# A graph-attention and expert-layer kernel: the fourth block loaded among the first, chains of blocks 3 and 4 begun at turns 8 and 12, padding and biases written ahead of the first slots

## The chip, the core and the metric

The kernel runs on one core of a Trainium2 chip (trn2). The metric is the device time of one execution in microseconds. The profile's engines are PE (TensorE matmuls), PEld (TensorE weight loads), DVE (VectorE), ACT (ScalarE), POOL (GpSimd) and SP (SyncE, which issues most DMAs).

## The reference

Two layers over x of shape (128, 64, 256), 128 graphs of 64 nodes, with an adjacency per graph. Each layer is an attention over the nodes of a graph and then a layer of 8 experts of which each token takes two. Cut to what matters:

```python
# layer l; ln is a layer norm without weights
xn = ln(x); Wh = xn @ W
e  = (Wh @ a1)[:, :, None] + (Wh @ a2)[:, None, :]     # layer 1: leaky relu on e
att = softmax(where(adj > 0, e, -9e15))
x  = x + elu(att @ Wh)
t  = ln(x)
logits = t @ router                                     # layer 1: + bg + bias
w, idx = top2(logits), softmax over the two
# layer 0: x = x + (t + sum over the two experts of w * (gelu(t @ w1 + b1) @ w2 + b2))
# layer 1: x = x + sum over the two experts of w * (relu(t @ w1 + b1) @ w2 + b2)
```

The hidden width of an expert is 256 in layer 0 and 512 in layer 1. All data is fp32.

## The kernel before

The 8192 tokens are cut into 16 blocks of 512 tokens (TT = 4 tiles of 128 rows, 8 graphs) for each layer, so `blks` has 32 entries. A block passes through two Python generators that issue instructions up to each `yield`.

`attend` (blocks `a`): statistics of the layer norm on DVE (L225 to L228), the power `rs` on POOL (L230), the mask `cap` from the adjacency on POOL (L277), the normalised `xn` on ACT (L238), its transposes `pt` on PE (L249) and their copies `xt` (L253 on DVE, L255 on ACT), `pw` and its copy `wh` (L288, L295), `sm` (L299), the scores `pe` and `ee` (L307 to L323), the exponentials (L326), their division, the transposes `pp` and copies `pT` (L339, L340), the product `po` and its exponential `ex` (L346, L354), and `xb` (L360, L363).

`route` (blocks `r`): statistics again, `tn` (L238), its transposes, the router's product `pl` (L417), the copy `lg` (L426), the two largest, the residual scaled in place (L433) and written to `mid` by a DMA that POOL issues (L437), the position `ix` of each token in the list of its two experts (L477 to L492), eight scatters of rows to `lists` in HBM, issued by POOL (L497), and the `plan` of the next slots (L537 to L594).

A slot is 256 rows of one expert's list. `fetch` loads it (`xg`, L609), `weights` loads the expert's weights and biases (`wc`, L651, L655, L659, the last from `bcat`), and the slot's `x` (transposes L680, copy L684), `h` (L749, L757) and `y` (L777, L785, a scatter to `res` at L791) do the expert's work. `rest_of_lists` writes padding rows at the end of the lists (eight DMAs a layer, L850). `gather_biases` loads a layer's biases to `tb` (L206, L212) and `put_biases` writes them to `bcat` (L218).

The order is written out by hand. PE, DVE, ACT and SP run their instructions in the order in which the program issues them (`manual_schedule` over `ORDERED`); POOL's order is chosen by the framework, and each engine runs its own queue in order. The start loads blocks 0 to 2, then runs a loop of turns: in each turn, each chain whose turn has come issues its next stage. A chain of a block has 11 entries of attention (12 stages) and then the stages of the route:

```python
chains = [
    (0, att(0)[3:] + [(r, 0)] * 10),
    (1, att(1)[2:] + [(r, 1)] * 10),
    (2, att(2) + [(r, 2)] * 10),
    (11, att(FIRST) + [(r, FIRST)] * 2),
    (20, [(a, FIRST + 1)] * 3),
]
```

With FIRST = 3, block 0's `ix` is issued at turn 15 and its scatters at turn 16; those of blocks 1 and 2 follow at turns 17/18 and 20/21. Behind the turns `slots.fetch()` loads the first four slots, and the main loop over blocks begins, in which the stages of three blocks and the slots are interleaved. Tiles come from pools with a number of buffers for each tag; a tile of a tag waits until the buffer that it takes has been read for the last time. The tag `xs` has 3 buffers, `yb` (which `tb` uses too) has 2, `cap`, `ee` and `adj` have 3.

Of the kernel before, what the change touches and what calls it, by code (L numbers as in the profile page):

```python
# [8 lines left out]
F32 = mybir.dt.float32  # L9
I32 = mybir.dt.int32  # L10
# [6 lines left out]
P = 128  # L17
NG = 64
D = 256
KD = D // P  # L20
E = 8
TT = 4
# [13 lines left out]
def adj_ffn_kernel(  # L36
# [40 lines left out]
    FIRST = 3  # L77
# [11 lines left out]
    work = ctx.enter_context(tc.tile_pool(name="work", bufs=3))  # L89
# [21 lines left out]
    def part(b):  # L111

        return int(b >= CUT)
# [10 lines left out]
    for g in range(2):  # L124
        r = slice(g * NG, (g + 1) * NG)
# [30 lines left out]
    def load_gw(l):  # L156
        gw.append(const.tile([P, KD, D + 2], F32, name=f"gw{l}"))
        av.append(const.tile([P, KD, 2], F32, name=f"av{l}"))
        nc.sync.dma_start(
            out=gw[l][:, :, 0:D], in_=gnn_w[l].rearrange("(k p) f -> p k f", p=P)  # L160
        )
        nc.sync.dma_start(out=av[l], in_=gnn_a[l])

    def make_gw(l):
        wt = work.tile([P, KD, D], F32, tag="xt", name=f"wt{l}", bufs=2)
        for o in range(KD):
            pt = ps_c.tile([P, D], F32, tag="a", name=f"pwt{l}_{o}")
            for k in range(KD):
                nc.tensor.transpose(
                    pt[:, k * P : (k + 1) * P], gw[l][:, k, o * P : (o + 1) * P], ident  # L170
                )
            nc.scalar.copy(wt[:, o, :], pt)
        for k in range(KD):
            pa = ps_c.tile([P, 2], F32, tag="a", name=f"pa{l}_{k}")
            for o in range(KD):
                nc.tensor.matmul(
                    pa,
                    lhsT=wt[:, o, k * P : (k + 1) * P],
                    rhs=av[l][:, o, :],
                    start=(o == 0),  # L180
                    stop=(o == KD - 1),
                )
            nc.scalar.copy(gw[l][:, k, D : D + 2], pa)
# [4 lines left out]
    def load_router():  # L188
        for l in range(2):
            nc.sync.dma_start(out=rw[l], in_=router[l].rearrange("(k p) e -> p k e", p=P))  # L190
        nc.sync.dma_start(out=gb2[:, 0, :], in_=bg.partition_broadcast(P))
        nc.sync.dma_start(out=gb2[:, 1, :], in_=gbias.partition_broadcast(P))

    def counted(name, shape, pattern, base, mult):
        ti = work.tile(shape, I32, tag="cap", name=f"{name}_i")
        nc.gpsimd.iota(ti, pattern=pattern, base=base, channel_multiplier=mult)
        t = const.tile(shape, F32, name=name)
        nc.vector.tensor_copy(t, ti)
        return t

    def gather_biases(l):

        tb = work.tile([P, E, D + HC[l]], F32, tag="yb", name=f"tb{l}", bufs=2)
        nc.sync.dma_start(  # L206
            out=tb[:, :, 0:D],
            in_=b2[l].rearrange("e d -> (e d)").partition_broadcast(P).rearrange(
                "p (e d) -> p e d", e=E
            ),  # L210
        )
        nc.sync.dma_start(out=tb[:, :, D : D + HC[l]], in_=b1[l])  # L212
        if l == 0:
            nc.vector.tensor_scalar(tb[:, :, 0:D], tb[:, :, 0:D], -2.0, None, ALU.add)
        return tb

    def put_biases(l, tb):
        nc.sync.dma_start(out=bcat[l].rearrange("e p d -> p e d"), in_=tb)  # L218
# [611 lines left out]

    def load_block(l, b, first=None):

        xs = work.tile([P, TT, D], F32, tag="xs", name=f"xs{l}_{b}")
        yb = None
        nc.sync.dma_start(out=xs, in_=(mid_t if l else x_t)[b])
        if first:
            first()
        if l:
            yb = work.tile([P, TT, 2 * D], F32, tag="yb", name=f"yb{l}_{b}", bufs=2)
            nc.sync.dma_start(out=yb, in_=res_t[part(b)][b])  # L840
        ai = work.tile([P, TT, NG], I32, tag="adj", name=f"adj{l}_{b}")
        nc.sync.dma_start(out=ai, in_=adj_t[b])
        return xs, yb, ai


    def rest_of_lists(l):

        for e in range(E):
            r = E * CAP + e * SL
            nc.sync.dma_start(  # L850
                out=lists[l][r : r + SL, :].rearrange("(t p) d -> p t d", p=P),
                in_=pad[:, :, 0 : ROW[l]],
            )

    slots = Slots()
    blks = [{"l": l, "b": b} for l in range(2) for b in range(NB)]

    def there(i):
        return 0 <= i < len(blks) and blks[i]

    def load(i, first=None):
        if there(i):
            k = blks[i]
            if k["l"]:
                assert all(s["l"] or s["part"] != part(k["b"]) for s in slots.all[slots.ny :])
            k["in"] = load_block(k["l"], k["b"], first)
            k["a"] = attend(k["l"], k["b"], k)

    def a(i, n=1):
        if there(i):  # L870
            for _ in range(n):
                next(blks[i]["a"], None)

    def r(i, n=1):
        if there(i):
            k = blks[i]
            if "r" not in k:
                k["r"] = route(k["l"], k["b"], k)
            for _ in range(n):
                next(k["r"], None)  # L880
# [5 lines left out]
    load(1)  # L886
    load(2)
    load_router()
    a(0, 2)
    make_gw(0)  # L890
    a(0)
    a(1, 2)
    token2 = counted("token2", [P, NT], [[2 * P, NT]], 0, 2)
    token = counted("token", [P, NT], [[P, NT]], 0, 1)
    place = counted("place", [P, ST], [[P, ST]], 0, 1)
    att = lambda b: [(a, b)] * 9 + [(a, b, 2), (a, b)]
    chains = [
        (0, att(0)[3:] + [(r, 0)] * 10),
        (1, att(1)[2:] + [(r, 1)] * 10),
        (2, att(2) + [(r, 2)] * 10),  # L900
        (11, att(FIRST) + [(r, FIRST)] * 2),
        (20, [(a, FIRST + 1)] * 3),
    ]
    turn = 0
    while any(c for _, c in chains):
        for first, chain in chains:
            if turn >= first and chain:
                stage, *what = chain.pop(0)
                stage(*what)
        if turn == 2:  # L910
            places = counted("places", [P, SL], [[1, SL]], 0, 0)
            steps = counted("steps", [P, KS], [[SL, KS]], 0, 0)
            snum = counted("snum", [P, SF], [[1, SF]], 0, 0)
            tb0 = gather_biases(0)
        if turn == 5:
            put_biases(0, tb0)
            load_gw(1)
        if turn in (6, 8, 11):
            load(FIRST + (turn - 6) // 2)
        if turn == 11:  # L920
            make_gw(1)
        turn += 1
    slots.fetch()
    for t in range(FIRST, len(blks)):
        n = t + 1
        more = slots.nf - slots.ny > SB or len(slots.all) - slots.ny > SB
        if t + 3 != NB:
            load(t + 3)
        if t == FIRST:
            put_biases(1, gather_biases(1))  # L930
            rest_of_lists(0)
        if t == FIRST + 1:
            rest_of_lists(1)
        a(n)
        h()
        x()
        a(n)
        r(t - 1)
        a(n)
        h()  # L940
        r(t)
        slots.fetch()
        if more:
            x()
        a(n)
        r(t)
        if t + 2 != NB:
            a(t + 2)
        y()
        a(n)  # L950
        (h if more else x)()
        r(t)
        a(n)
        y()
        a(t + 2, 1 + (t + 2 == NB))
        if more:
            x()
        a(n)
        r(t)
        h()  # L960
        a(n)
        if more:
            y()
        x()
        a(n)
        h()
        r(n)
        y()
        a(t + 2)
        r(t)  # L970
        r(t)
        y()
        slots.fetch()
        x()
        r(n)
        r(t)
        if t + 3 == NB:
            load(t + 3)
# [57 lines left out]
```

## Time and profile before

| what | value |
|---|---|
| time, median of 3 runs | 1467.6 us (1464.61 to 1468.28) |
| the profiled execution's own time | 1464.47 us |
| its span | 1462.6 us |
| mean granted TensorE clock | 0.956 |
| DMA | 315.42 MB, mean 216 GB/s |
| scatters to `lists` (L497) | 256, mean 975 ns |
| first and last scatter of blocks 0 to 2 | 77.72 and 108.36 us |
| first fetch of slots (L609) | 110.99 us |
| first expert matmul (L749) | 138.66 us |

The profile is of one execution; its times are microseconds from the start of the span. A matmul's line has its output tile, its inputs, and its shape; the text in brackets at the end of a line of the timeline is how long the engine had been idle and what it waited for. PE is busy for 86% of the span; in the first 111 us it is busy for 66.86 us.

### The profile page before, as it was taken

How to read it: one execution, taken by the hardware profiler on the slowest of the kernel's cores; microseconds unless marked ns; L12 is line 12 of the kernel's file. 1: busy time of each engine (PE TensorE's matmuls, PEld its weight loads, DVE VectorE, ACT ScalarE, POOL GpSimd, SP SyncE). 2: the span in 40 equal slices, each digit the busy share in tenths (PEclk: the TensorE clock that was granted, in tenths of full speed). 3: DMA queues.
4: the chain of work that ended last, by engine and by line, in shares of the span. 5: the costliest groups of instructions: out<-in, count | busy, mean ns of one | idle time of the engine just before them, and what ended most of it. 6: DMA issues, size and time to landing. Idle time of an engine off the chain costs nothing. (4 is left out here: it accounts for less than half of the span.)

```text
span 1462.6 us, 22822 instructions
## 1 busy us (share of the span) xinstructions
PE 1264.9 (86%) x6436; PEld 1082.9 (74%) x6436; DVE 885.6 (61%) x3404; ACT 670.3 (46%) x1567; POOL 767.8 (52%) x742
## 2 busy tenths in 40 slices
PE   6646789889989888888889999899988998899996
PEld 4534677777777777777778887777877787688885
DVE  3663777776677678677766655666566655423332
ACT  5523556546655554545444444344444443233232
POOL 3261566656565555555563654555645465544333
PEclk9766999989999999999999999999999999999999
DMA  4228766697666779777786987898877778987773
GB/s 128 83 98 266 240 209 219 210 279 233 214 216 210 268 253 271 260 240 235 240 254 183 265 238 205 220 263 223 228 195 215 209 193 212 241 248 215 214 178 57
DMA packets 267199, 315.42 MB, mean 216 GB/s; under 512 B 41400, under 2 KB 224319, under 8 KB 267073
## 3 DMA queue, kind: packets, MB, share of 16 engines
q1 hardware_dynamic: 222240, 227.80, 51.3%
q0 software_dynamic: 44832, 86.17, 22.0%
q8 instruction: 51, 0.84, 0.2%
q14 instruction: 76, 0.61, 0.1%
HBM read 215.03 MB, written 102.51 MB: 217 GB/s over the span
## 5 line engine op out<-in xcount | busy, mean ns | idle before, releaser
L749 PE MATMUL ph_s<-xT_s,wc_s 128*128 128x256 f32 x1760 | 418.9, 388 | 71.1 <-DVE xT_s L684 49.3
L749 PEld LDWEIGHTS ph_s<-xT_s,wc_s 128*128 128x128 f32 x1760 | 333.4, 193 | 135.1 <-DVE xT_s L684 66.6
L777 PE MATMUL py_s<-wc_s,hT_s 128*128 128x256 f32 x1760 | 417.1, 387 | 14.9 <-issue 14.6
L777 PEld LDWEIGHTS py_s<-wc_s,hT_s 128*128 128x128 f32 x1760 | 331.4, 193 | 59.9 <-issue 17.2
L820 POOL DMA_INDIRECT out_dram<-ys_s,to_s x142 | 223.1, 1571 | 273.2 <-ACT ys_s L817 170.3
L497 POOL DMA_INDIRECT lists<-tn_r,ix_r x256 | 249.5, 975 | 110.9 <-issue 66.1
L757 ACT ACTIVATE hT_s<-ph_s,wc_s 128x256 f32<-128x256 f32 x440 | 182.3, 469 | 176.8 <-PE ph_s L749 88.1
L785 DVE TENSOR_TENSOR ys_s<-py_s,wc_s 128x512 f32<-128x512 f32 x149 | 102.9, 691 | 196.1 <-PE py_s L777 184.5
L791 POOL DMA_INDIRECT res<-ys_s,to_s x156 | 159.0, 1019 | 117.4 <-DVE ys_s L785 51.6
L684 DVE COPY xT_s<-px_s 128x512 f32<-128x512 f32 x149 | 102.3, 686 | 118.1 <-PE px_s L680 118.1
L817 ACT ACTIVATE ys_s<-ys_s,cf_s 128x256 f32<-128x256 f32 x142 | 64.1, 499 | 141.1 <-DVE ys_s L785 134.8
L288 PE MATMUL pw_g<-gw,xt_g 128*128 128x258 f32 x512 | 125.5, 395 | 1.7 <-ACT wh_g L295 1.3
L288 PEld LDWEIGHTS pw_g<-gw,xt_g 128*128 128x128 f32 x512 | 95.8, 196 | 22.8 <-ACT xt_g L255 6.3
L238 ACT ACTIVATE xn_g<-xs,nb_g,rs_g 128x256 f32<-128x256 f32 x128 | 66.4, 589 | 82.0 <-DVE nb_g L236 82.0
L238 ACT ACTIVATE tn_r<-xb_g,nb_r,rs_r 128x256 f32<-128x256 f32 x128 | 66.4, 589 | 66.8 <-DVE nb_r L236 66.8
L680 PE MATMUL px_s<-ident,xg_s 128*128 128x128 f32 x596 | 90.9, 276 | 0.5 <-DMA xg_s<-lists 0.5
L680 PEld LDWEIGHTS px_s<-ident,xg_s 128*128 128x128 f32 x596 | 74.9, 145 | 13.0 <-DMA xg_s<-lists 0.6
L277 POOL TENSOR_SCALAR cap_g<-adj 128x256 f32<-128x256 int32 x32 | 35.7, 1117 | 91.6 <-DMA adj<-in_adj_dram 90.2
L346 PE MATMUL po_g<-wh_g,pT_bd 128*128 128x256 f32 x256 | 69.0, 417 | 7.4 <-ACT pT_bd L340 5.8
L295 ACT COPY wh_g<-pw_g 128x258 f32<-128x258 f32 x128 | 47.7, 374 | 54.2 <-PE pw_g L288 53.2
L417 PEld LDWEIGHTS pl_r<-rw,xt_r 128*128 128x128 f32 x512 | 68.1, 207 | 2.9 <-DVE xt_r L253 0.6
L230 POOL TENSOR_TENSOR rs_r<-ve_r,nhalf 128x4 f32<-128x4 f32 x32 | 38.3, 1198 | 57.1 <-DVE ve_r L228 50.4
(474 smaller groups left out, 1597.8 us busy)
## 6 DMA issues: line engine op xcount, KB each, us to landing
wc_s<-in_w_dram SPq DMA_DIRECT2D x142, 512.0 KB, 4.3
wc_s<-in_w_dram SPq DMA_DIRECT2D x156, 256.0 KB, 3.9
xg_s<-lists SPq DMA_DIRECT2D x78, 258.0 KB, 4.3
xg_s<-lists SPq DMA_DIRECT2D x71, 260.0 KB, 4.4
yb<-res SPq DMA_DIRECT2D x16, 1024.0 KB, 10.5
wc_s<-bcat SPq DMA_DIRECT2D x78, 129.0 KB, 3.8
wc_s<-bcat SPq DMA_DIRECT2D x71, 130.0 KB, 5.3
xs<-in_x_dram SPq DMA_DIRECT2D x16, 512.0 KB, 6.1
```

Source lines behind the costliest of these rows:

```text
L238: nc.scalar.activation(outs(t), xb[:, t, :], AF.Identity, bias=nb[:, t : t + 1], scale=rs[:, t : t + 1])
L288: nc.tensor.matmul(pw, lhsT=xt[:, k, t * P : (t + 1) * P], rhs=gw[l][:, k, :], start=(k == 0), stop=(k == KD - 1),)
L346: nc.tensor.matmul(po[h][:, j, :], lhsT=pT[:, 2 * h + j, :], rhs=wh[:, 2 * h + j, 0:D], start=True, stop=True,)
L497: ins = nc.gpsimd.indirect_dma_start(out=lists[l], out_offset=bass.IndirectOffsetOnAxis(ap=ix[:, k, t : t + 1], axis=0), in_=tn[:, t, 0 : ...
L680: nc.tensor.transpose(px[:, c, t * P : (t + 1) * P], xg[:, t, c * P : (c + 1) * P], ident)
L684: nc.vector.tensor_copy(xT, px)
L749: nc.tensor.matmul(ph[:, j, :], lhsT=wc[:, o : o + P], rhs=xT[:, c, :], start=(c == 0), stop=(c == KD - 1),)
L757: nc.scalar.activation(hT[:, f + j, :], ph[:, j, :], AF.Gelu if l == 0 else AF.Relu, bias=wc[:, OB1[l] + f + j : OB1[l] + f + j + 1],)
L777: nc.tensor.matmul(py[:, t, :], lhsT=hT[:, f, t * P : (t + 1) * P], rhs=wc[:, O2[l] + f * D : O2[l] + (f + 1) * D], start=(f == 0), stop=( ...
L785: nc.vector.tensor_tensor(ys, py, wc[:, OB2[l] : OB1[l]].unsqueeze(1).to_broadcast([P, ST, D]), ALU.add)
L791: ins = nc.gpsimd.indirect_dma_start(out=res[sl["part"]], out_offset=self.row(sl, t), in_=ys[:, t, :], in_offset=None, bounds_check=2 * N - 1,
L820: ins = nc.gpsimd.indirect_dma_start(out=out, out_offset=self.row(sl, t), in_=ys[:, t, :], in_offset=None, compute_op=ALU.add,)
```

## The change

Block 3's input and adjacency are loaded behind the first three blocks' instead of at turn 6; its `xs` takes a buffer of the tag `yb`. Blocks 4 and 5 are loaded at turns 6 and 8 (before: 8 and 11). The chain of block 3 begins at turn 8 instead of 11, that of block 4 at turn 12 instead of 20. The last stage of block 2's route (its plan) is issued behind the turns. The biases of layer 1 are loaded and written at turn 5, and the padding of both layers at turn 11; before, both stood in the first two rounds of the main loop. The weights of the first four slots are issued straight behind the first fetch (`slots.ahead()`). The small integer tiles of `counted` take buffers of `ee` instead of `cap`.

```diff
     def counted(name, shape, pattern, base, mult):
-        ti = work.tile(shape, I32, tag="cap", name=f"{name}_i")
+        ti = work.tile(shape, I32, tag="ee", name=f"{name}_i")
...
     def load_block(l, b, first=None):
-        xs = work.tile([P, TT, D], F32, tag="xs", name=f"xs{l}_{b}")
+        tag, bufs = ("yb", 2) if l == 0 and b == FIRST else ("xs", 3)
+        xs = work.tile([P, TT, D], F32, tag=tag, name=f"xs{l}_{b}", bufs=bufs)
...
     load(2)
     load_router()
+    load(FIRST)
...
-        (2, att(2) + [(r, 2)] * 10),
-        (11, att(FIRST) + [(r, FIRST)] * 2),
-        (20, [(a, FIRST + 1)] * 3),
+        (2, att(2) + [(r, 2)] * 9),
+        (8, att(3) + [(r, 3)] * 2),
+        (12, [(a, 4)] * 3),
...
-            tb0 = gather_biases(0)
+            tb = gather_biases(0)
         if turn == 5:
-            put_biases(0, tb0)
+            put_biases(0, tb)
             load_gw(1)
-        if turn in (6, 8, 11):
-            load(FIRST + (turn - 6) // 2)
+            tb = gather_biases(1)
+            put_biases(1, tb)
+        if turn in (6, 8):
+            load(4 + (turn - 6) // 2)
         if turn == 11:
             make_gw(1)
+            for l in range(2):
+                rest_of_lists(l)
         turn += 1
+    r(2)
     slots.fetch()
+    slots.ahead()
...
-        if t == FIRST:
-            put_biases(1, gather_biases(1))
-            rest_of_lists(0)
-        if t == FIRST + 1:
-            rest_of_lists(1)
```

## The prediction

> **What bounds the kernel now.** I read the page first, then a table by stage, the list of waits, and the timeline of the start.
>
> ```profile
> span 1462.6 us, 22822 instructions
> PE 1264.9 (86%) x6436; PEld 1082.9 (74%) x6436; DVE 885.6 (61%) x3404; ACT 670.3 (46%) x1567; POOL 767.8 (52%) x742
> ```
>
> TensorE carries the kernel. By stage (columns: stretch, length, busy time of PE, PEld, DVE, ACT, POOL, granted clock, DMA share, GB/s):
>
> ```profile
> 0.00:111.00 111.00, 66.86 (x268) 50.99 (x268) 59.47 (x251) 49.00 (x126) 48.82 (x102) 0.77 0.34 103
> 111.00:150.00 39.00, 27.44 (x112) 20.83 (x113) 17.34 (x67) 16.30 (x39) 5.90 (x7) 0.70 0.93 278
> 200.00:400.00 200.00, 177.90 (x934) 151.30 (x933) 145.46 (x562) 113.40 (x251) 124.90 (x126) 0.97 0.77 239
> ```
>
> From 200 us on PE is busy 89% of the time; the first 150 us leave it idle for 56 us. Only this start is changed; behind it the order on every engine is the same in both kernels, and nothing is tied to absolute time. So the change is worth the shift of one fixed point: the first expert matmul, ph of slot 0, at 138.66. The waits in 95 to 140 us (engine, line, waited for: us, times, longest):
>
> ```profile
> PE pt_g L249 <- ACT xn_g L238: 13.6, 1, 13.6
> PE ph_s L749 <- DMA wc_s<-in_w_dram: 6.4, 1, 6.4
> POOL mid L437 <- ACT xb_g L433: 5.4, 1, 5.4
> ```
>
> The timeline (start, duration, what) shows how these arise:
>
> ```profile
> 67.66 0.19 DVE L426 COPY lg_r<-pl_r 128x32 f32<-128x32 f32 x1 [1.86 <-PE pl_r L417]
> ...
> 77.72 1.11 POOL L497 DMA_INDIRECT lists<-tn_r,ix_r  x1 [5.26 <-DVE cs L466]
> ...
> 108.36 0.96 POOL L497 DMA_INDIRECT lists<-tn_r,ix_r  x1 [0.30 <-issue]
> ...
> 109.34 1.05 POOL L230 TENSOR_TENSOR rs_g<-ve_g,nhalf 128x4 f32<-128x4 f32 x1
> ...
> 110.99 3.07 SPq L609 DMA_DIRECT2D xg_s<-lists  x4
> ...
> 114.01 5.67 PE L288 MATMUL pw_g<-gw,xt_g 128*128 128x258 f32 x16
> ...
> 123.65 9.29 SPq L850 DMA_DIRECT2D lists<-pad  x8
> ...
> 128.47 3.78 PE L346 MATMUL po_g<-wh_g,pT_bd 128*128 128x256 f32 x8 [1.84 <-ACT pT_bd L340]
> ...
> 138.66 3.38 PE L749 MATMUL ph_s<-xT_s,wc_s 128*128 128x256 f32 x8 [6.40 <-DMA wc_s<-in_w_dram]
> ```
>
> GpSimd issues 24 scatters of blocks 0 to 2, one each 1.27 us, from 77.72 to 109.3 (24 x 1.27 = 30.5, and one write of mid). Block 4's rs (L230) stands behind them, so xn and PE wait: the 13.6 us. Then SP has block 6's loads, tb1, bcat1 and eight pads ahead of the first weights, which leave at 134.15: the 6.4 us.
>
> **The change, part by part.** *Early load of block 3.* xs3 and adj3 go out at about 9.6 and 10 us instead of 37.36; they delay tb0 by 0.66 MB, about 3 us at 222 GB/s. tb0 was down by 15 and its L214 ran at 19.36: 0. The load was not late before either (its first reader ran at 63.4). What it buys is that the xs buffers freed at 37.3 and 45.1 now go to blocks 4 and 5.
>
> *tb1 and bcat1 early.* tb1 takes tb0's buffer, so SP stands until bcat0 has landed (issued 20.60; the DMA rate falls after 25), then about 6 us as tb0 took: bcat1 leaves at 32 to 33. Behind it on SP is xs4, which waits for its buffer until 37.3 anyway: 0; each us past 37.3 would hold adj4 and with it cap4 and rs of block 0 on POOL.
>
> *Sixteen pads at 46 us,* behind adj5. They hold SP until some 62 us and the DMA for 4.1 MB / 0.3 MB per us = 14 us; nothing else there is urgent but adj5, which cap5 needs and behind which rs of blocks 3 and 1 stand on POOL. adj loads land in 3.9 us; 6.1 are free before DVE would wait. [...] the pads' own landings under saturation were 5.9 and 7.6 in the median, 8.0 at most, which would cost 1.9. I take 0, bounds 0 and 1.9. On GpSimd the iotas in other buffers let cap2 move ahead of rs of block 1: about 1 us late, with 4 us of room before its xn at 17.84: 0.
>
> *Chains 3 and 4 at turns 8 and 12.* This is the cost. The first scatter needs ix of block 0 (turn 15). Ahead of it now stand block 3's stages to exp (before: to its transposes) and block 4's statistics and xn. Walking the queues from 48.6, where the two orders part:
> - DVE: block 3's statistics first (2.4), so pT of block 2 is at 53.4 instead of 52.24. ACT: then xn of block 3 (2.07) ahead of tn of block 1 and ex of block 2: ex at 60.4 instead of 58.85, the first L360 done at 61.7.
> - PE from 61.75: block 3's transposes 2.1, make_gw 2.4 (as at 60.20), pt_r 1.4, pw of block 3 4.9 (as at 77.48), pl of block 1 1.85 (with gaps): ends at 74.4 instead of 67.63.
> - DVE waits for that pl, then works without a pause: lg group 1.3, statistics of blocks 2 and 4 at 2.42 each, sm 0.45, c group 0.58, second choice 1.59, nb 0.3, ee and emx 0.9, at to ix 2.1: 12.1. ix at 86.5, first scatter at **86.6: 8.9 late**.
>
> *What this buys.* rs of block 4 is ahead of all scatters and rs of block 3 behind 16 of them: 86.6 + 20.4 + one write of mid 1.1 = 108.1. DVE stands there at nb of block 3 (109.3), then does the plan (3.7): xt of block 4 at 113.2, pw at 113.95, as before (114.01). So the 13.6 us wait only moves. Scatters end at 86.6 + 32.7 = 119.3, the fetch leaves at 121.0, slot 0 lands 4.1 later: px at 125.1 instead of 123.4. But DVE reached xT only at 125.37 before; now 125.75, so po ends at 132.7. Weights leave from 124.4 and land by 129.6. ph starts at **132.7**: 6.0 earlier. All is the removed weight wait.
>
> *The clock.* In windows of ten us the clock was
>
> ```profile
> 50.00:60.00 10.00, 9.01 (x34) 7.61 (x33) 3.15 (x15) 6.64 (x13) 2.75 (x3) 0.52 0.15 52
> 130.00:140.00 10.00, 3.60 (x9) 2.43 (x8) 1.71 (x4) 1.41 (x4) 1.03 (x1) 0.50 1.01 292
> ```
>
> [...] By it the dense stretch from 61.75 runs at full rate (pw 3.83, pl 1.85, pt 1.04): pl ends at 72.3, first scatter 84.4, and ph of slot 0, behind po without a gap, takes 1.99 instead of 3.38: 8.2 + 1.4 = 9.6 gained. The row at 50 to 60 speaks against it: 9.0 us busy, clock 0.52. Were all of it so (pt 2.31, pw 5.67, pl 3.42), pl ends at 78.0, first scatter 90.2, gain 2.4. I take the middle walk and half of the 1.4: **6.7 us gained**.
>
> The tail of r(2) behind the loop is the same instructions; the fetch needs the scatters, 6 us after the plan: 0. The second eight pads leave the stretch from 143, where PE was 0.9 busy: 0.
>
> The sum is against the profiled execution: 1464.5 (span 1462.6 and 1.9 around it) to 1457.8. That is one of the fast ones; the median of the three is 1467.6, so I forecast 1467.6 - 6.7 = **1460.9**. A difference of 0.3% (4.4 us) is about what a measurement of this kernel can tell from no change.
>
> **Rivals.** *B, the early stages are hidden.* From 40 to 77 us (the windows of ten us added up) PE was idle for about 11 us, ACT for 16 and DVE for 14. If they fit into that, the first scatter stays near 77.7 and ph comes at 77.7 + 46.1 = 123.8: 14.9 + 1.4 = 16.3 gained, 1451.3. Against it: the queues are in order, and pw stands in front of pl.
>
> *C, the gain is given back.* The half clock of the row at 50 to 60, or a late ix of block 1 (slack 1.2 us to its scatters): 0 to 4.4 gained, about 1465.
>
> *D, slower: none of it is hidden.* The added stages ahead of ix of block 0 at full latency: statistics and rs 3.4, xn and transposes 2.9, xt 0.7, pw 5.3, sm 0.45, pe 1.2, ee and emx 0.9, exp 2.1, block 4's statistics, rs and xn 5.5: 22.4. First scatter at 100, ph at 146: 7.5 lost, 1475. It decides from a first scatter at 97.0. For it: POOL, DVE and ACT hand each stage on, so latencies count. Against it: much of block 4's part is not read in that stretch.
>
> *E, the change does not do what it says.* Chains 3 and 4 do start earlier on all queues, but the load is no cure: the transfer of block 3 was hidden already. That is inside A and C.
>
> **How the numbers follow.** A (4.4 to 10 gained) 0.50; B and between (over 10) 0.17; C 0.20; D 0.13. Faster 0.67, same 0.20, slower 0.13. A's own range is 1457 to 1463. The range for 8 in 10 takes in B's end and C: 1451 to 1467; outside are D and a little beyond B.
>
> **What would show it.** First L497 at 84 to 90 instead of 77.72; last one at 117 to 123; PE idle before pt or pw of block 4 still above 10 us; no wait of ph on wc; ph of slot 0 at 130 to 134; pads at 46 to 62. I am wrong if the first scatter stays below 82 or passes 92, if POOL waits for adj5 beyond 51.7, or if ph shifts by 6 us and the span does not.

## The result and the profile after

| | before | after |
|---|---|---|
| time, median | 1468.09 us (5 runs, 1464.61 to 1471.29) | 1455.54 us (5 runs, 1452.59 to 1456.64) |
| the profiled execution's own time | 1464.47 us | 1454.15 us |
| its span | 1462.6 us | 1452.2 us |
| mean granted TensorE clock | 0.956 | 0.960 |

The ratio is 0.9918, with a 95% interval of 0.9903 to 0.9934: about 12 us faster, 10 to 14 by the interval. A second comparison of the changed kernel, run with the last experiments, gave 1454.64 us (5 runs, 1453.25 to 1457.95) against 1467.24, ratio 0.9920 (0.9906 to 0.9935). The forecast was 1460.9 us, in a range of 1451 to 1467.

The head of the page of the changed kernel, and PE's longest wait in its first 140 us (engine, line, waited for: us in total, times, longest):

```profile
span 1452.2 us, 22826 instructions
PE 1264.1 (87%) x6436; PEld 1083.9 (75%) x6436; DVE 884.4 (61%) x3404; ACT 670.1 (46%) x1567; POOL 767.2 (53%) x742
```

```profile
PE pw_g L288 <- DVE xt_g L253: 13.0, 1, 13.0
```

No engine does less work; PE's busy time differs by 0.8 us in 1264. The 13 us wait of PE for block 4 is still there and only has another name: pw waits for xt on DVE, where pt waited for xn. The 6.4 us wait of ph for the weights is gone from the list. The timeline of the changed kernel shows both:

```profile
46.62 13.31 SPq L852 DMA_DIRECT2D lists<-pad  x16
...
74.28 0.19 DVE L426 COPY lg_r<-pl_r 128x32 f32<-128x32 f32 x1 [8.59 <-PE pl_r L417]
...
85.91 1.10 POOL L497 DMA_INDIRECT lists<-tn_r,ix_r  x1 [4.17 <-DVE ix_r L492]
...
107.03 1.05 POOL L230 TENSOR_TENSOR rs_r<-ve_r,nhalf 128x4 f32<-128x4 f32 x1
...
108.12 0.16 DVE L236 SCALAR_TENSOR_TENSOR nb_r<-mv_r,rs_r 128x4 f32<-128x4 f32 x1 [2.40 <-POOL rs_r L230]
...
112.98 6.16 PE L288 MATMUL pw_g<-gw,xt_g 128*128 128x258 f32 x16 [13.02 <-DVE xt_g L253]
...
117.19 0.96 POOL L497 DMA_INDIRECT lists<-tn_r,ix_r  x1 [0.30 <-issue]
...
119.98 3.09 SPq L609 DMA_DIRECT2D xg_s<-lists  x4
...
123.62 0.38 SPq L651 DMA_DIRECT2D wc_s<-in_w_dram  x1
...
127.80 3.78 PE L346 MATMUL po_g<-wh_g,pT_bd 128*128 128x256 f32 x8 [1.85 <-ACT pT_bd L340]
...
131.37 1.99 PE L749 MATMUL ph_s<-xT_s,wc_s 128*128 128x256 f32 x8
```

Before, SP issued the biases (from 115.17) and eight pads between the fetch and the weights:

```profile
115.17 0.50 SPq L206 DMA_DIRECT2D tb<-in_b_dram  x1
...
134.15 0.40 SPq L651 DMA_DIRECT2D wc_s<-in_w_dram  x1
```

Everything up to the fetch is later than before: the first scatter by 8.2 us (77.72 to 85.91), the fetch by 9.0 (110.99 to 119.98). Yet the weights leave 10.5 us earlier (134.15 to 123.62), since neither biases nor padding lie between the fetch and them, and ph of slot 0 starts at 131.37 instead of 138.66, straight behind po and with no wait of its own. That is 7.3 us. It also took 1.99 us instead of 3.38, at a mean granted clock of 0.95 instead of 0.58 over its run. At slot 1 the changed kernel is 8.7 us ahead, at the last slot 10.3, which is the difference of the two spans (10.4).

### The profile page after: what moved, and what is told of

Read it like the earlier page. It is cut to its first block, busy times and chain, and to the rows that moved or that the text cites. A ratio compares the mean times of both kernels' runs of the same rounds, so it can differ in the third digit from the quotient of the medians.

```text
span 1452.2 us, 22826 instructions
## 1 busy us (share of the span) xinstructions
PE 1264.1 (87%) x6436; PEld 1083.9 (75%) x6436; DVE 884.4 (61%) x3404; ACT 670.1 (46%) x1567; POOL 767.2 (53%) x742
## 5 line engine op out<-in xcount | busy, mean ns | idle before, releaser
L288 PEld LDWEIGHTS pw_g<-gw,xt_g 128*128 128x128 f32 x512 | 96.7, 197 | 35.1 <-issue 13.2
L417 PE MATMUL pl_r<-rw,xt_r 128*128 128x8 f32 x512 | 63.5, 259 | 2.9 <-ACT xt_r L255 2.5
## 6 DMA issues: line engine op xcount, KB each, us to landing
yb<-res SPq DMA_DIRECT2D x16, 1024.0 KB, 10.2
```

The costliest lines, as they stand in the source:

```text
L288: nc.tensor.matmul(pw, lhsT=xt[:, k, t * P : (t + 1) * P], rhs=gw[l][:, k, :], start=(k == 0), stop=(k == KD - 1),)
L417: nc.tensor.matmul(pl[:, t, :], lhsT=tT[:, k, t * P : (t + 1) * P], rhs=rw[l][:, k, :], start=(k == 0), stop=(k == KD - 1),)
```

## Experiments

All were timed in five rounds beside runs of the kernel before on the same chip. The table gives the end points; "shift" is how far ahead of the profile of before the copy xT of a slot stands (slot 1, and the last; slots are counted from 0). Each profile is of one execution, so a shift need not match its ratio: the profile of the writes only took 1461.37 us, where the median is 1456.54.

| kernel | ratio (95% interval) | first scatter | weights leave | ph of slot 0 | shift, us |
|---|---|---|---|---|---|
| before | 1 | 77.72 | 134.15 | 138.66 | 0, 0 |
| changed | 0.9918 (0.9903 to 0.9934) | 85.91 | 123.62 | 131.37 | 8.7, 10.3 |
| changed, again | 0.9920 (0.9906 to 0.9935) | 86.71 | 124.26 | 132.10 | 8.0, 9.8 |
| writes only | 0.9915 (0.9893 to 0.9938) | 79.41 | 116.25 | 132.99 | 6.0, 3.2 |
| chains only | 1.0045 (1.0028 to 1.0062) | 86.19 | 143.03 | 150.25 | -12.4, -10.4 |
| biases only | 0.9921 (0.9898 to 0.9943) | 77.86 | 124.44 | 132.55 | 7.5, 8.9 |
| padding only | 0.9920 (0.9900 to 0.9941) | 77.89 | 114.50 | 131.08 | 8.1, 8.6 |
| weights first | 0.9933 (0.9912 to 0.9954) | 84.80 | 111.37 | 132.92 | 6.8, 11.1 |
| block 4 ahead | 0.9975 (0.9962 to 0.9988) | 85.45 | 109.68 | 132.94 | 5.1, 0.6 |
| block 3 at turn 9 | 0.9890 (0.9870 to 0.9911) | 82.13 | 121.14 | 128.07 | 10.9, 11.4 |
| block 3 at turn 10 | 0.9903 (0.9878 to 0.9927) | 84.70 | 122.78 | 129.50 | 10.6, 12.2 |
| block 4 early | 0.9896 (0.9881 to 0.9911) | 81.12 | 120.73 | 124.70 | 13.2, 11.8 |
| block 4 early, weights first | 0.9920 (0.9907 to 0.9934) | 80.98 | 108.60 | 125.06 | 11.2, 11.8 |

### The two halves of the change apart

Writes only: the kernel before, with the biases, the padding and the first weights where the changed kernel has them (the padding at turn 8, not 11), and its own loads and chains.

```diff
         if turn == 5:
             put_biases(0, tb0)
             load_gw(1)
+            put_biases(1, gather_biases(1))
+        if turn == 8:
+            for l in range(2):
+                rest_of_lists(l)
...
     slots.fetch()
+    slots.ahead()
...
-        if t == FIRST:
-            put_biases(1, gather_biases(1))
-            rest_of_lists(0)
-        if t == FIRST + 1:
-            rest_of_lists(1)
```

> Before, with only the writes moved: biases of layer 1 at turn 5, padding of both layers at turn 8, first weights straight behind the first fetch; load and chains of blocks 3 and 4 as before. Theory W (the moved writes carry the gain, the early chains none of it): first list scatter at 77 to 79 us, the wait of PE for block 4's xn of some 13 us stays, no wait of ph on wc, ph of slot 0 at 131 to 133 us, time 8 to 11 us below before (ratio 0.9925 to 0.9945). Rival C (the early chains carry it): ph of slot 0 above 135 us and at most 3 us gained.

Chains only: the changed kernel with exactly these writes put back into the main loop, and no `slots.ahead()` behind the fetch.

> After, with the writes put back where before has them (biases of layer 1 and padding in the first rounds of the main loop, weights behind them); block 3 loaded early and chains 3 and 4 at turns 8 and 12. Theory W: first list scatter at 86 us, fetch at 120, then block 6's loads, biases, eight pads on SP, so that the first weights leave at about 143 and ph of slot 0 comes at 147 to 149: 8 to 10 us slower than before (ratio about 1.006). Rival C: ph of slot 0 below 133, 5 us or more gained.

Measured: 1456.54 us for the writes, 1474.78 for the chains, against 1467.66. The timeline of the kernel with the writes only, from PE's wait for block 4 to ph:

```profile
112.85 2.80 PE L249 MATMUL pt_g<-ident,xn_g 128*128 128x128 f32 x8 [13.60 <-ACT xn_g L238]
...
132.99 3.00 PE L749 MATMUL ph_s<-xT_s,wc_s 128*128 128x256 f32 x8
```

The same 13.6 us wait as before, and ph has none. The waits and the timeline of the kernel with the chains only:

```profile
PE ph_s L749 <- DMA wc_s<-in_w_dram: 18.4, 1, 18.4
```

```profile
134.01 7.97 SPq L852 DMA_DIRECT2D lists<-pad  x8
...
143.03 0.40 SPq L651 DMA_DIRECT2D wc_s<-in_w_dram  x1
...
150.25 3.78 PE L749 MATMUL ph_s<-xT_s,wc_s 128*128 128x256 f32 x8 [18.44 <-DMA wc_s<-in_w_dram]
```

So all of the gain is the writes', and the early chains alone lose 6.6 us (0.0045 of 1467.7). The two runs also show why the loss does not show in the whole change. Where the queue behind the fetch sets ph, the chains' delay of the fetch (9.6 here, 120.60 against 110.99) reaches ph: it came 11.6 later, since the weights left 8.9 later and took 2.7 longer from there to ph. With the writes away, ph is set by PE's own chain, pw of block 4 to po, and the place of pw hardly moves with the chains (its rs stood behind 24 scatters, and now nb of block 3 stands behind 16 later ones): pw starts at 114.01, 112.98, 113.74 and 113.60 in before, changed, changed again and chains only. A delay of the fetch is then covered.

### Which of the writes

Biases only moves the line `put_biases(1, gather_biases(1))` of the kernel before to turn 5 and nothing else. Padding only moves both layers' padding to turn 8, and the first weights behind the fetch:

```diff
+        if turn == 8:
+            for l in range(2):
+                rest_of_lists(l)
...
     slots.fetch()
+    slots.ahead()
...
         if t == FIRST:
             put_biases(1, gather_biases(1))
-            rest_of_lists(0)
-        if t == FIRST + 1:
-            rest_of_lists(1)
```

> The kernel before with only the biases of layer 1 (gather and put) at turn 5; padding, weights, loads and chains as before. Theory W (the weights were 6.4 us late behind 18.9 us of bias and padding issues, so taking away either part of 8.5 us or more ends the wait): weights leave at about 125.7 (134.15 before), the first ph at 132 to 133 with no wait or one under 1 us, time 5 to 7 us below before, as with both parts moved but for the second layer's padding. Rival (the two parts each carry their share of the gain): ph at 135 to 136, time about 3 us below before.

> The kernel before with only the padding of both layers at turn 8, and the weights issued ahead of the main loop, behind the first fetch; biases of layer 1, loads and chains as before. bcat of layer 1 then stands behind the weights of the first slots for the layer 0, and only its own wait is left for what follows. Theory W: weights leave at about 116, the first ph at 132 to 133 with no wait, time 5 to 8 us below before, within 3 us of the kernel that moves both. Rival (the biases' wait of 5.2 us ahead of bcat then stops the queue in front of the next weights or the next fetch): ph of slot 0 without a wait but that of a later slot with one, and less than half of the gain left by slot 8.

Measured: 1456.52 and 1456.98 us against 1468.31. Moving the biases alone gives the whole gain. The second run gives it too, but it does not take the padding alone out of the way: `slots.ahead()` puts the first weights in front of the biases as well. It shows that the biases cost nothing once they stand behind these weights; what moving the padding alone would bring was not run. SP's queue with the biases moved, and then ph:

```profile
118.19 5.04 SPq L850 DMA_DIRECT2D lists<-pad  x8
...
124.44 0.39 SPq L651 DMA_DIRECT2D wc_s<-in_w_dram  x1
...
132.55 1.97 PE L749 MATMUL ph_s<-xT_s,wc_s 128*128 128x256 f32 x8
```

The wait to be removed was 6.4 us, and each half holds more: from the first bias DMA to the first pad SP spent 8.5 us (115.17 to 123.65), and from the first pad to the weights 10.5 (123.65 to 134.15). Once ph stands behind po, taking more out of SP's queue buys nothing: weights at 114.50 or at 124.44 give ph at 131.08 and 132.55. In the kernel with the padding moved, the biases' stop of 6 us (bcat1 leaves at 133.19, the loads before it were issued by 127.16) stands behind the weights and holds up block 7's load and nothing that is waited for: the shift is 8.1 us at slot 1 and 8.2 at slot 20. The rival, that it comes back in a later slot, is refuted.

### What is last in the changed kernel

Weights first: the changed kernel with `slots.ahead()` in front of `slots.fetch()`.

> After, with the first four slots' weights issued ahead of the first fetch. Theory W and Q: the weights are already down when ph of slot 0 becomes ready behind po of block 4, so ph stays at 131 and the time within 1.5 us of after. Rival: the weights still decide, and ph comes 2 us or more earlier. The rows of the slots land no later, since the fetch waits for the scatters.

Measured: 1457.71 us, no difference from the changed kernel that the intervals show. The weights left 12 us earlier, the fetch 1.6 later (121.62), and px now waited for it:

```profile
125.08 1.11 PE L680 MATMUL px_s<-ident,xg_s 128*128 128x128 f32 x4 [3.42 <-DMA xg_s<-lists]
```

The weights are not last any more. Block 4 ahead attacks the other candidate, the 13 us wait: the rest of block 4's attention and the first route stages of block 3 are issued before the fetch.

```diff
-        (8, att(3) + [(r, 3)] * 2),
+        (8, att(3) + [(r, 3)]),
...
+    a(4)
     r(2)
-    slots.fetch()
     slots.ahead()
+    r(3)
+    a(4, 3)
+    r(3)
+    a(4)
+    r(3)
+    a(4)
+    r(3)
+    a(4, 3)
+    slots.fetch()
```

> After, with block 4's remaining attention and block 3's first route stages issued in front of the first fetch instead of in the main loop's first round, the first weights ahead of the fetch, and block 3's normalisation behind the plan. Theory Q (what still holds PE at 100 to 113 us is the order of DVE's queue, where nb of block 3, waiting for its power behind 16 scatters, stands in front of the plan and of block 4's xt): that wait of 13 us goes, px of slot 0 runs as soon as its rows land at about 123, ph at 124 to 125, 5 to 8 us below after (some 17 to 20 below before). Rival S (the scatters on GpSimd set the pace anyway, and the second fetch gives it back): ph of slot 0 earlier, but the span not more than 2 us below after.

Measured: 1463.79 us, 8 slower than the changed kernel. The wait did shrink, and nothing came of it:

```profile
105.86 3.78 PE L288 MATMUL pw_g<-gw,xt_g 128*128 128x258 f32 x8 [6.38 <-DVE du_p L537]
...
129.03 1.06 PE L680 MATMUL px_s<-ident,xg_s 128*128 128x128 f32 x4
...
132.94 1.99 PE L749 MATMUL ph_s<-xT_s,wc_s 128*128 128x256 f32 x8 [2.16 <-DVE xT_s L684]
```

px now stands behind po in PE's order, so ph waits for xT. Worse, the order of what follows changed: slots 4 to 7 were 14 to 21 us ahead, but pn of block 4 came at 179.0 us (161.6 in the changed kernel), the third fetch at 197.51 (before: 199.46), and the lead was 1.6 us at slot 8 and 0.5 from slot 9 on. The expectation took the wait for the price; it was only where the time showed.

### Where the 8 us of the scatters come from

The prediction named pw of block 3, ahead of pl of block 1 in PE's order. Block 3 at turn 9 begins that chain a turn later and takes its last three attention steps at once, so that its route stages keep their turns:

```diff
-        (8, att(3) + [(r, 3)] * 2),
+        (9, [(a, 3)] * 9 + [(a, 3, 3)] + [(r, 3)] * 2),
```

Block 3 at turn 10 is `(10, [(a, 3)] * 8 + [(a, 3, 4)] + [(r, 3)] * 2)`.

> The changed kernel with the chain of block 3 begun at turn 9 in place of 8, and its last three attention steps taken in one turn, so that its two route stages stay at turns 19 and 20 and rs of block 3 stays between the scatters of blocks 1 and 2. In TensorE's order pl of block 1 now stands before pw of block 3, and pn of block 0 before pe of block 3. Theory D (pw of block 3, 4.9 us long ahead of pl of block 1, is what made the first scatter 8 us later): first scatter at 81 to 82 (85.91 in the changed kernel, 77.72 before), rs and nb of block 3, xt and pw of block 4 and the first ph earlier by the same 4 us (ph at about 127.5 against 131.4), and the time 3 to 4 us below the changed kernel's. Rival D2 (the delay is VectorE's and ScalarE's share of block 3's attention, spread over the stretch): first scatter at 85 to 86 still, time within 1 us of the changed kernel's. Rival D3 (scatters earlier, but the 8 PE-side steps put off come back in front of ph): scatters earlier by 4, ph at 131, time the same.

> As the kernel with the chain at turn 9, but begun at turn 10 and with the last four attention steps of block 3 in one turn; route stages at turns 19 and 20. Now pl of block 1 stands before pt and pw of block 3, and xn of block 3 behind more of the routing. Theory D: first scatter at 79 to 81, ph of slot 0 at 125 to 127, time 4 to 6 us below the changed kernel's. Rival D4 (block 3's po, with four steps bunched at turn 18, is then late and holds pn of block 2 and so the last scatters): first scatter early, but the last at 117 to 118 as in the changed kernel, and no gain over it.

Measured: 1452.67 and 1453.88 us. The timeline at turn 9:

```profile
67.81 3.42 PE L417 MATMUL pl_r<-rw,xt_r 128*128 128x8 f32 x16
...
71.08 6.09 PE L288 MATMUL pw_g<-gw,xt_g 128*128 128x258 f32 x16
...
82.13 1.10 POOL L497 DMA_INDIRECT lists<-tn_r,ix_r  x1 [3.72 <-DVE ix_r L492]
...
110.08 5.37 PE L288 MATMUL pw_g<-gw,xt_g 128*128 128x258 f32 x16 [10.01 <-DVE xt_g L253]
...
128.07 3.09 PE L749 MATMUL ph_s<-xT_s,wc_s 128*128 128x256 f32 x8
```

The first scatter comes 3.8 us earlier, the wait of PE shrinks by 3.0, ph starts 3.3 earlier, at the stations and about in the sizes that theory D gave; D2 and D3 fall. Of the 3.3, 1.1 go again because ph took 3.09 us, at a granted clock of 0.50 until about 130.5. So about half of the chains' 8 us goes with the later start of block 3. That it is pw's place alone is read from PE's order and not shown, since the same edit takes three attention steps in one turn. One turn later the theory's numbers fail: with pt and pw of block 3 both behind pl, the first scatter came at 84.70, not 79 to 81. PE's timeline at turn 10:

```profile
71.99 3.38 PE L288 MATMUL pw_g<-gw,xt_g 128*128 128x258 f32 x8 [2.54 <-DVE xt_g L253]
78.77 3.41 PE L288 MATMUL pw_g<-gw,xt_g 128*128 128x258 f32 x8 [3.39 <-ACT wh_g L295]
82.01 0.31 PE L474 MATMUL pn_r<-mm_r,before 128*128 128x32 f32 x2
```

The second half of pw waited for ACT's copy of the first, which ACT did only at 78.36, behind another block's tn, for whose nb it had stood 6.3 us. And pn of block 0, without which there is no ix, stands behind pw in PE's order. DVE stood 6.0 us waiting for that pn. So pw still delayed the scatters, from another place and by ACT's order. Rival D4 isn't it: the late part is the first scatter, not the last ones.

### Two more steps of block 4

Block 4 early is the kernel at turn 9 with one more entry, `(19, [(a, 4)] * 2)`: xt and pw of block 4 ahead of nb of block 3. The other kernel has `slots.ahead()` in front of the fetch as well.

> The kernel with block 3's chain at turn 9 (128.07 for the first ph), with two more steps of block 4's attention, the transposes with xt and pw, taken at turns 19 and 20, ahead of nb of block 3 in VectorE's order; the fetch, the weights and the order of the first slots stay. It undoes TensorE's wait of 10.0 us for xt of block 4 without the reordering of the earlier try with block 4 ahead. Theory P (that wait is on the path to po and ph): pw of block 4 before 104, po ends before px at about 117, and the first ph is then bound by px and the weights, at about 125.5, but behind a gap[...]: slot 1 about 2 to 3 us ahead of the kernel without it, time about 1450. Rival P2 (the weights, issued at 121.1, land at about 125.5 and the gap's slow ph eats what is won): slot 1 within 1 us, time the same. Rival P3 (given back as in the earlier try, by the order of the later slots): ahead at slot 1, level by slot 8.

> As the kernel with two more early steps of block 4, and the first slots' weights issued ahead of the first fetch: they left at 111.4 when this was tried alone, and the fetch 1.6 us later. If the weights bound the first ph of the other kernel: ph at about 123.5 to 124.5, 1 to 2 us ahead of it, time 1 us less. Rival: the fetch's 1.6 us of delay comes straight through px, time the same or 1 us more.

> The changed kernel itself, on the same chip and beside the same runs of the kernel before as the two others. If its gain is what the first comparison gave: ratio 0.990 to 0.994. Its profile is a second drawing of the clock: the first ph, 1.99 us in the first profile, may take up to 3.4; the first scatter should be at 85.9 and the first ph at 131.4 within 0.5 us again, and slot 1 7.3 to 8.7 us ahead of the kernel before.

Measured: 1452.79, 1455.78 and 1454.64 us. The timeline with block 4 early:

```profile
102.63 3.78 PE L288 MATMUL pw_g<-gw,xt_g 128*128 128x258 f32 x8 [3.70 <-DVE at_r L477]
...
120.35 0.60 PE L680 MATMUL px_s<-ident,xg_s 128*128 128x128 f32 x4
...
124.70 3.75 PE L749 MATMUL ph_s<-xT_s,wc_s 128*128 128x256 f32 x8 [3.76 <-DMA wc_s<-in_w_dram]
...
130.09 3.75 PE L749 MATMUL ph_s<-xT_s,wc_s 128*128 128x256 f32 x8 [0.78 <-DVE xT_s L684]
```

po was done before px, and ph started 3.4 us ahead of the kernel at turn 9 (128.07), but behind a gap, waiting for the weights again. Both first ph then took 3.75 us instead of 3.09 and 1.99; the lead over that kernel is 2.3 us at slot 1, as theory P had it, but 0.5 at slot 2 and 0.4 at the end. What rival P2 put at slot 1 came one slot later: the longer runs of the two ph took 0.7 and 1.8 us of the gain, and the time stayed the same. With the weights in front, the first slot's rows left 2.5 us later (119.06 against 116.54) and ph started at 125.06: nothing won. Its median is 3 us above, and the intervals overlap.

The kernel at turn 9 has the lowest median, 2.9 us under the first one of the changed kernel and 2.0 under the second. Its interval (0.9870 to 0.9911) still overlaps theirs (0.9903 to 0.9935), so it beats the kernel before, and whether it beats the changed one is likely but not settled.

## Why the prediction was right, and where its sizes were off

The direction, the mechanism and the range held: case A came in, and rivals B and D did not.

- *First scatter at 86.6, 8.9 late.* Measured 85.91 and 86.71. The walk through the queues held at its stations: ex of block 2 at 60.4 (60.23), PE from 61.75 (61.59), pl of block 1 ends at 74.4 (the copy behind it ran at 74.28), ix at 86.5 (85.6). Rival B (first scatter near 77.7) and rival D (100, decisive from 97.0) both fall by this one line.
- *"The 13.6 us wait only moves."* It did: rs of block 3 at 108.1 (107.03), nb at 109.3 (108.12), pw of block 4 at 113.95 (112.98).
- *ph at 132.7, 6.0 earlier.* 131.37, 7.3 earlier; 132.10 in the second profile, 6.6. The fetch left at 119.98 (121.0 predicted), 0.7 of it because the scatters began earlier. px came 2.8 us behind the fetch, not 4.1, but po ended last in any case: at 131.6, not 132.7.
- *"All is the removed weight wait."* Confirmed by the writes alone and the chains alone. What the prediction did not see is that the biases alone would have done, and that the chains are a loss of their own wherever the fetch's queue sets ph.
- *Biases and sixteen pads at nothing.* They were: SP was held from 46.62 to 59.9 (46 to 62 predicted), bcat1 left at 31.45 (32 to 33). adj5, issued at 46.12 ahead of the pads, was read at 50.37, 4.25 us later, in time for the 51.7 that the prediction had set as the limit. That pads issued behind a load do not hold it up was the author's estimate; this one load shows no rule. With the writes alone the first scatter came 1.7 later (79.41); why is not shown, and the ratio shows no loss. (In rival B, DVE's idle time from 40 to 77 us adds up to 13 us, not 14; nothing rests on it.)
- *The clock, half of 1.4.* This term was a draw, not a size. ph behind po took 1.99 and 1.98 us in the two profiles of the changed kernel, so all of 1.4 came there; that the stretch from 61.75 could run at the full rate was the author's estimate, and it did not (last section). In other kernels with no gap ahead of ph it took up to 3.09 (block 3 at turn 9).

The forecast of 6.7 us was low against the 12 of the ratio. Step by step the profiles give 7.3 for ph's start (6.6 again), 1.4 for its clock, and 0.6 where a later ph behind block 5's transposes ran faster (2.69 us instead of 3.29; the granted clock rose from 0.50 to 1.00 about 1.4 us into it instead of 2.6): 9.3 at slot 5. Another 2.3 came between slots 20 and 28, 1.9 in the second profile, nearly all of it between slots 21 and 22. There too it is the clock, at the same work: the scores pe and the router's pl of one block, first before, then changed.

```profile
315.62 1.22 PE L307 MATMUL pe_g<-sm_g,same 128*128 128x256 f32 x2 [2.34 <-DVE sm_g L299]
...
317.48 3.42 PE L417 MATMUL pl_r<-rw,xt_r 128*128 128x8 f32 x16
```

```profile
306.77 0.70 PE L307 MATMUL pe_g<-sm_g,same 128*128 128x256 f32 x2 [2.34 <-DVE sm_g L299]
...
307.74 2.21 PE L417 MATMUL pl_r<-rw,xt_r 128*128 128x8 f32 x16
```

By the traces the granted clock stood at 0.50 for 10.2 us there in before (from 315.6) and for 6.8 in both profiles of the changed kernel (from 309.1 in the first, 0.99 on average from 306.77 to there). With biases only and at turn 9 it was 3.4 us, and the step is 2.6 and 2.8; with writes only, padding only or block 4 early it was 10.2 as in before, and the step is at most 0.2. So the 2.3 us is the clock's. Whether other executions of a kernel have it, one or two profiles of each do not show. Since writes only and padding only have ratios like the changed kernel's without it, it can't be read as a part of the medians' difference.

The other 2 us between the profiles' 10.3 and the medians' 12 lie inside the interval: the profiled execution of before is 3.6 us under its median, that of the changed kernel 1.4 under its own. Why executions differ so was not tested. What failed in the forecast is not its mechanism but a size: it took the fixed point's shift as the whole, with half of the 1.4 for the clock at ph, and put the clock behind that point at nothing. In the profiles ph's start gave 7.3 where 6.0 stood, its clock 1.4 where 0.7 stood, and the clock behind it 0.6 and then 2.3.

## What to carry to other kernels

When a transfer is late, look at what stands in front of it in its issuing queue before making its inputs earlier: here moving one round trip of the biases out of the way gave the whole gain. A wait list names one wait at a time; take the second one in line (po behind pw of block 4) as the ceiling, since anything beyond it is not paid. An early start that delays a queue is free only while another chain ends later, so test the parts apart: of this change one half was a gain of 11 us and the other, by itself, a loss of 7.

## What the runs showed of the hardware

How fast ph ran behind po differed from run to run with the same work in front. In windows of two microseconds (columns as in the tables by stage; the clock is the third number from the right), first the changed kernel, then block 3 at turn 9, then padding only:

```profile
131.00:133.00 2.00, 2.00 (x10) 1.73 (x9) 0.92 (x2) 1.37 (x3) 0.00 (x0) 0.86 1.09 374
```

```profile
129.00:131.00 2.00, 2.00 (x8) 1.59 (x7) 0.63 (x1) 1.28 (x2) 0.00 (x0) 0.63 0.89 286
```

```profile
131.00:133.00 2.00, 2.00 (x6) 1.56 (x5) 0.69 (x1) 1.66 (x3) 0.14 (x1) 0.50 0.72 178
```

po and ph run without a pause from 127.80, 124.49 and 127.50. A clock of 0.50 that turns to 1.00 inside the window gives 0.86 or 0.63 on average, so it turned near 131.6 and 130.5 in the first two, and near 133.1 in the third (0.92 on average from 133.00 to 133.50): about 3.8, 6.0 and 5.6 us after po began. What sets this time is not shown.

The prediction weighed a walk with the stretch from 61.75 at the full rate against one with all of it at half. In the changed kernel the granted clock there was 0.82 from 62 to 64 us, 0.50 from 64 to 70, 0.97 from 70 to 72 and 1.00 from 72 to 74; pw took 4.85 us, between the 3.83 and 5.67 of the two walks and near the 4.9 of the middle one. From 50 to 60 us, the row that the prediction used, PE works in the changed kernel from 49.77 to 59.27 without a pause, at half clock, and the clock turns only as PE falls idle:

```profile
56.00:58.00 2.00, 2.00 (x6) 1.57 (x5) 1.02 (x7) 2.00 (x5) 0.00 (x0) 0.50 1.11 275
58.00:60.00 2.00, 1.27 (x3) 0.46 (x2) 0.00 (x0) 2.00 (x5) 1.03 (x1) 0.53 1.09 278
60.00:62.00 2.00, 0.41 (x4) 0.42 (x4) 1.16 (x2) 1.29 (x3) 0.00 (x0) 1.00 1.10 314
```

```profile
52.23 3.42 PE L417 MATMUL pl_r<-rw,xt_r 128*128 128x8 f32 x16
...
55.51 3.76 PE L346 MATMUL po_g<-wh_g,pT_bd 128*128 128x256 f32 x8
```

The clock turned at about 59.9, 4.4 us after po began. In front of po stand transposes and the router's pl, matmuls with 8 output columns; while they ran, from 50 to 55.5 us, the clock was 0.50. These runs give such times for single stretches; a rule for when the clock turns is not shown.

The other surprise is the price of issuing: eight pads took SP 9.29 us before, 7.97 with the chains only, and 5.04 with the biases moved, so the same eight instructions cost 0.6 to 1.2 us each. What sets the price is not shown.
